# A decoder layer on one core: attention maxima by blocks of 64 queries for two heads at once, and two small stages taken through memory

## The chip, the cores and the metric

The kernel runs on one core of one Trainium2 chip. The metric is the device time of one execution in microseconds, from three executions without a profiler; a separate execution was taken with the hardware profiler, and every duration below that is not one of those three times comes from it. Engines are named as the profile names them: PE is the matmul engine, DVE the vector engine, ACT the scalar engine, POOL the general engine, and SP the queue that issues most of the transfers.

## The reference

One decoder layer works on x of 16 batches, 128 rows and 512 columns, in three sub-layers, each with a residual and a LayerNorm behind it. The retention part takes the 128 rows of a batch as the sequence. In the cross part a batch is read as 512 positions with 128 features. The last part picks 16 of the 128 rows of each batch.

```python
# 1. retention, 16 heads of 32, by batch
Q, K, V = (einsum('bsh,nhd->bnsd', X, W) for W in (W_Q, W_K, W_V))
ret = einsum('bnsd,bntd->bnst', xpos(Q), xpos(K, inverse)) * D      # D: gamma^(n-m), causal
Y = einsum('bnst,bntv->bnsv', ret, V)
Yn = (Y - mean) / sqrt(var + 1e-5) * gn_weight + gn_bias            # mean, var by head and row
x = layernorm(x + (silu(X @ W_G) * Yn) @ W_O)
# 2. banded attention over 512 positions, 8 heads of 16, |i - j| <= 64
scores = where(band, einsum('bqhd,bkhd->bhqk', q, k) / 4, lowest)
o = einsum('bhqk,bkhd->bqhd', softmax(scores), v) @ w_out.T + b_out
x = layernorm(x + relu(o).T * ctx @ w_ct + b_ct)
# 3. mixture of depths: 16 rows of each batch by score, then attention and MLP on those 256 rows
_, idx = top_k(einsum('btd,d->bt', x, w_router), 16); idx = sort(idx)
sel = x[b, idx]                                     # 256 rows
x1 = sel + causal_attention(rms_norm(sel))          # 16 heads, 8 key heads, rotary by idx
processed = x1 + (silu(h2 @ w_gate) * (h2 @ w_up)) @ w_down
x = layernorm(x.at[b, idx].set(gate * processed + (1 - gate) * sel))
```

## The kernel before, in words

All matmuls are fp32. Each shows as two records in the trace, so a count of records is twice the count of matmuls in the code.

**Three stages.** Retention goes by group, two batches at a time (8 groups). The cross part goes by batch, and inside a batch by unit: a unit is one batch with four of its eight heads (32 units; `m` is `2 * n + hg`). When retention has ended, the weights of the last part are loaded into a ring of six tiles, and that part runs on the 256 chosen rows.

**The order.** Each step is a generator with stages between its `yield`s. The tables `PLACES`, `ENDS`, `FIRST` and `ONCE` give a time to every stage of every step, and `in_order` sorts them into one order of the program. `FF_PLACES` does this for the last part. Each engine and each queue runs its own instructions strictly in that order, so the tables only decide what stands ahead of what.

**PSUM.** There are eight banks, handed out by `bank()` in rotation. The call that comes eighth after another gets its bank again, and waits until it has been read.

**The steps that matter here.** `scores` (steps `s0`, `s1`) computes, for a unit, the scores of two of the four chunks of 128 queries against the 192 or 256 keys in their band, for four heads in the four strips of 32 rows of PE. DVE adds the band and keeps the maximum of each query (L788): one instruction for one chunk and one head, so 8 behind each step and 16 for a unit. `lower` (step `low`) turns the maxima round and puts them, as one more feature, into the free rows of the queries `x_qT`: for batches 2 to 12 (`IN_MEMORY`) through two transfers, for batches 0, 1, 13, 14 and 15 by four transposes on PE (`xmx_ps`) from `wide_mxs`, which DVE has written directly. `weights` (steps `w0`, `w1`) then computes the transposed scores less their maxima, ACT takes the exponential (L829), and POOL cuts the band out (L835). `attend` (step `av`) multiplies with the values, `divide` and `turn` divide by the sums, `project_out` and `settle` finish the batch and write the score of each row.

In retention `variance` (step `var`) makes one divisor for each row and head. `normalise` (step `norm`) spreads it over the 32 features of a head by eight small matmuls into four banks (`spread_ps`, L708) and applies weight, bias and gate in eight DVE instructions (L712, L714). `finish` (steps `O0`, `O1`) multiplies by W_O.

`rank` counts, for each row of a batch, how many scores are above it: PE spreads the scores over the partitions by a transpose (`rank_ps`, L949), DVE compares and counts, a matmul with `after` numbers the chosen rows (`slot_ps`, L960), and DVE writes a 0/1 matrix into `wide` (L964), with which `gather` picks rows on PE.

At the start, SP issues the weights and, among the loads that follow, 25 small ones of the cross part; POOL issues only the four transfers of the decay table; the table `xpos` comes on ACT's queue.

Of the kernel before, what the change touches and what calls it, by code (L numbers as in the profile page):

```python
# [14 lines left out]
P = 128  # L15
# [6 lines left out]
GB = 2  # L22
# [12 lines left out]


IN_MEMORY = range(2, 13)
FREE = (XD, 0)
# [16 lines left out]
for _k, _w in _W.items():  # L55
# [7 lines left out]
    "q": [(-1.5107, 0.5513), (-1.4314, 0.6844)],  # L63
    "k": [(-1.51, 0.6571), (-1.4782, 0.7507)],
    "s0": [(-1.2644, -0.8382, 1.0251, 1.8751)],
    "s1": [(-0.6502, -0.1387, 1.1361, 2.4268)],
    "low": [(-0.452, 0.2528, 1.4558, 2.6592), (-0.3388, 0.255, 1.477, 2.6843)],
    "w0": [(0.351, 0.9575, 1.9746, 3.1188), (0.6532, 1.3693, 2.8463, 3.2972)],
    "w1": [(0.1628, 1.8596, 2.3575, 3.7432), (0.8299, 2.0241, 2.8359, 3.8093)],
    "av": [(1.0536, 2.2471, 3.077, 4.2619)],  # L70
    "div": [
        (1.549, 2.3132, 3.3032, 4.5514),
        (2.1607, 2.8293, 3.6961, 4.7908),
        (2.2814, 2.9057, 4.2425, 4.8691),
        (2.7316, 3.2963, 4.2834, 5.4207),],
    "v": [(-0.7717, 1.6867)],
    "enc": [(4.2298, 5.8947)],
    "turn": [(3.7073, 5.9438)],
    "out": [(5.5379, 6.1922), (5.6383, 6.7827)],
    "settle": [(5.7824, 7.2066), (6.1581, 7.7192), (6.2045, 8.378), (6.8636, 9.2875)],  # L80
    "rank": [(8.8254, 11.7601), (10.5726, 15.5543), (14.3738, 16.7912)],
    "load": [(-10.091,)],
    "Q0": [(-8.0888,), (-7.0032,)],
    "K0": [(-9.2641,), (-7.4284,)],
    "V0": [(-7.4999,)],
    "Q1": [(-6.8478,), (-6.0577,)],
    "R0": [(-6.7213,), (-6.147,)],
    "K1": [(-6.3248,), (-4.7817,)],
    "V1": [(-5.4583,)],
    "Y0": [(-5.0578,)],  # L90
    "G0": [(-4.829,), (-4.8109,)],
    "R1": [(-4.766,), (-4.6504,)],
    "G1": [(-4.5788,), (-4.5641,)],
    "Y1": [(-4.274,)],
    "var": [(-4.1573,), (-3.7966,)],
    "norm": [(-3.5102,)],
    "O0": [(-3.0724,), (-2.8181,), (-2.079,)],
    "O1": [(-2.0994,), (-0.2461,), (-0.0548,)],
# [4 lines left out]
        "q": [(-14.5047, -14.0322), (-9.6551, -10.8844)],  # L103
        "k": [(-14.6216, -0.0686), (-11.7977, 0.2659)],
        "s0": [(-10.3426, -9.3436, 0.6635, 1.6471)],
        "s1": [(-1.4102, -0.8775, 1.1056, 2.0571)],
        "low": [(-0.9192, 0.4442, 1.3301, 2.655), (25.4644, 25.2394, 26.846, 30.099)],
        "w0": [(-0.0687, 0.9881, 1.867, 3.6646), (0.6483, 1.0316, 2.1657, 3.801)],
        "w1": [(-0.716, 0.5784, 1.6289, 3.7788), (-0.1082, 0.8202, 2.3021, 4.2159)],
        "av": [(0.8022, 1.6738, 3.6998, 4.4162)],  # L110
        "div": [
            (1.3197, 2.3014, 3.8551, 4.5595),
            (9.3024, 12.4358, 15.7006, 13.259),
            (11.4285, 19.3987, 23.3186, 13.7145),
            (24.0753, 30.3386, 24.8529, 51.4762),],
        "v": [(-2.6646, -1.1793)],
        "enc": [(-25.1063, 5.5925)],
        "turn": [(3.2132, 5.214)],
        "out": [(3.4449, 5.6355), (4.2463, 5.7715)],
        "settle": [(4.6796, 7.6854), (5.8827, 7.8003), (6.6518, 8.4034), (6.7825, 8.7614)],  # L120
        "rank": [(8.7442, 12.5945), (11.2119, 15.6141), (14.4792, 18.3604)],
# [13 lines left out]
        "var": [(-3.6239,), (-3.5616,)],  # L135
        "norm": [(-3.4454,)],
        "O0": [(-3.0951,), (-2.9746,), (-2.0282,)],
        "O1": [(-2.7016,), (-2.0346,), (-1.7197,)],
    },
    1: {  # L140
        "q": [(-1.8166, -0.2185), (-1.7211, 0.2268)],
        "k": [(-1.4245, 0.5821), (-1.1045, 0.6675)],
        "s0": [(-1.1449, -0.3061, 1.1186, 0.88)],
        "s1": [(-0.7336, -0.1968, 1.3979, 1.5727)],
        "low": [(-0.299, 0.2134, 1.5144, 2.0884), (0.0557, 0.6188, 1.7807, 2.2233)],
        "w0": [(0.2707, 1.1081, 2.008, 3.7721), (0.3399, 1.2959, 2.8815, 3.7842)],
        "w1": [(0.4634, 0.7763, 2.1476, 3.124), (0.6199, 0.7887, 2.7228, 3.773)],
        "av": [(0.9363, 1.4927, 2.9839, 4.1957)],
        "div": [
            (0.9666, 1.6683, 3.2221, 4.4914),  # L150
            (1.3326, 2.19, 3.2714, 4.7046),
            (1.848, 2.4848, 3.3512, 5.1111),
            (2.0714, 3.0715, 4.4949, 5.7185),],
        "v": [(-2.1434, 1.2462)],
        "enc": [(2.2681, 6.6251)],
        "turn": [(3.7868, 6.1403)],
        "out": [(4.4181, 6.4823), (5.3138, 7.1825)],
        "settle": [(5.9958, 7.5759), (6.474, 7.966), (6.642, 8.7653), (7.2408, 8.9043)],
        "rank": [(10.0834, 11.6296), (12.019, 14.0816), (14.7883, 15.0275)],
        "load": [(-45.4451,)],  # L160
        "Q0": [(-40.5376,), (-31.555,)],
        "K0": [(-44.4545,), (-33.577,)],
        "V0": [(-28.6881,)],
        "Q1": [(-29.5172,), (-17.2537,)],
        "R0": [(-24.1539,), (-17.035,)],
        "K1": [(-32.7547,), (-24.7952,)],
        "V1": [(-13.608,)],
        "Y0": [(-9.3686,)],
        "G0": [(-20.8822,), (-15.6663,)],
        "R1": [(-7.9384,), (-5.8625,)],  # L170
        "G1": [(-8.5881,), (-7.538,)],
        "Y1": [(-5.1994,)],
        "var": [(-4.9466,), (-4.3898,)],
        "norm": [(-3.5502,)],
        "O0": [(-3.2591,), (-2.5035,), (-2.4622,)],
        "O1": [(-2.4561,), (-1.8438,), (-0.69,)],
    },
    6: {
        "q": [(-2.0548, 0.7039), (-2.0286, 0.9716)],
        "k": [(-1.5582, 0.6681), (-1.2975, 0.7797)],  # L180
        "s0": [(-1.1563, -0.4807, 0.9293, 1.876)],
        "s1": [(-0.9454, 0.0322, 1.3978, 2.4624)],
        "low": [(-0.5199, 0.3687, 1.8114, 2.9216), (0.1135, 0.7655, 6.6942, 8.7044)],
        "w0": [(0.619, 1.6449, 2.4026, 3.8245), (1.4903, 1.8685, 3.442, 3.9205)],
        "w1": [(0.4016, 1.312, 1.9452, 3.2547), (0.8685, 1.8118, 2.9524, 3.6025)],
        "av": [(1.5506, 2.0007, 3.7283, 4.366)],
        "div": [
            (1.7326, 2.5114, 4.5357, 5.4752),
            (2.3608, 3.0019, 14.1691, 12.0944),
            (2.6919, 3.5211, 32.2671, 26.848),  # L190
            (3.3016, 3.6721, 45.677, 30.3915),],
        "v": [(0.897, 3.5685)],
        "enc": [(3.2024, 5.2296)],
        "turn": [(3.8903, 5.8957)],
        "out": [(4.2266, 6.4601), (5.1506, 6.8067)],
# [14 lines left out]
        "Y1": [(-4.6408,)],  # L210
        "var": [(-4.088,), (-3.7221,)],
        "norm": [(-3.551,)],
        "O0": [(-3.1254,), (-3.0228,), (-2.9897,)],
        "O1": [(-2.7332,), (-2.301,), (-1.3014,)],
    },
    7: {
# [1187 lines left out]
```

## Time and profile before

| | |
|---|---|
| three executions without a profiler | 855.94, 855.16, 853.21 us; median 855.16 |
| the profiled execution | 857.26 us, of which the span from first to last instruction is 855.56 us |
| busy: PE, DVE, ACT, POOL | 825.2, 529.4, 384.8, 367.2 us |
| mean granted clock of PE | 0.987 |
| 50 to 548 us: PE busy | 497.6 of 498.0 us |
| 548 to 657.5 us: PE busy | 95.5 of 109.5 us |
| maxima on DVE (L788) | 512 of them, 424 ns for 256 columns and 357 ns for 192, each with a readout of 83 ns |

How to read it: a line of a group names the source line, the engine, the operation, what it writes and reads, the shape, how many records there are, how long they were busy together, the mean of one in ns, and the idle time of the engine just before them with what ended it. PE's records overlap, since matmuls are pipelined, so the cost of a step on PE is read from one start to the next. The span's parts are these: start to about 50 us, then retention and cross part interleaved until the last W_O matmul ends at 562.3 us, then the cross part alone until the second gather ends at 657.5 us, and then the last part.

### The profile page before, as it was taken

The page shows a single profiled execution, that of the slowest core. Times are in us where ns is not written, and L with a number is a line of the kernel's source. Part 1 is how long each engine was busy: PE and PEld are TensorE (multiplying, and loading weights), DVE is VectorE, ACT ScalarE, POOL GpSimd, SP SyncE. Part 2 cuts the span into 40 slices and gives each one's busy share as a digit, 9 for nine tenths or more (in the row PEclk, how much of TensorE's full clock was granted, in tenths as well). Part 3 has the DMA queues.
Part 4 walks back from the last instruction along what each step waited for, and adds up shares of the span by engine and source line. Part 5 has one row for each costly group of instructions (what it writes and reads, how often), then busy time and mean ns, then how long its engine had stood idle before and what let it go on. Part 6 is the DMA issues. An engine that isn't in the chain of part 4 may idle for free.

```text
span 855.6 us, 17846 instructions
## 1 busy us (share of the span) xinstructions
PE 825.2 (96%) x6762; PEld 571.1 (67%) x6762; DVE 529.4 (62%) x1793; ACT 384.8 (45%) x773; POOL 367.2 (43%) x527
## 2 busy tenths in 40 slices
PE   8999999999999999999999999988988999999996
PEld 6676767766766676587567657554554777658865
DVE  4644665677687678777787788877775276311112
ACT  0315634654473564546465456655443367421100
POOL 4634353364486554755654584644452121000001
PEclk9999999999999999999999999998899999999998
DMA  9500100003102110201211011138010633142500
GB/s 291 178 28 1 51 1 2 3 3 80 51 6 77 37 46 28 78 28 34 85 42 30 27 47 38 41 91 306 27 38 13 197 98 100 52 146 99 186 11 25
DMA packets 38373, 58.16 MB, mean 68 GB/s; under 512 B 10016, under 2 KB 13856, under 8 KB 38288
## 3 DMA queue, kind: packets, MB, share of 16 engines
q1 hardware_dynamic: 35552, 54.67, 19.9%
q10 hardware_dynamic: 2448, 1.58, 0.7%
q8 instruction: 53, 0.87, 0.4%
q0 software_dynamic: 288, 0.79, 0.3%
q14 instruction: 32, 0.26, 0.1%
HBM read 51.58 MB, written 5.44 MB: 67 GB/s over the span
## 4 chain that ended last, share of the span: by engine, by line
PE 81%; DVE 6%; issue 5%; DMA 3%; ACT 2%; POOL 1%; SPq 1%; POOLq 0%; DVEq 0%; ACTq 0%
PE xt_ps L824 7%; PE o_ps L722 7%; PE gu_ps L1248 7%; PE xs_ps L776 6%; PE xav_ps L846 6%; PE q_ps L604 6%; PE k_ps L604 6%; PE v_ps L623 6%; PE g_ps L632 6%; PE down_ps L1263 3%; PE wo_ps L1223 3%; PE xqk_ps L744 3%; PE xout_ps L904 2%; PE ret_ps L653 2%; PE xct_ps L914 2%
## 5 line engine op out<-in xcount | busy, mean ns | idle before, releaser
L788 DVE CUSTOM_DVE_ANT_0 x_masked<-xs_ps,x_band 128x192 f32<-128x192 f32 (+1 forms) x512 | 199.8, 390 | 73.0 <-PE xs_ps L776 34.0
L835 POOL TENSOR_SCALAR_AFFINE_SELECT xp_t<-xp_t 128x512 f32<-128x512 f32 (+1 forms) x256 | 146.2, 609 | 110.7 <-ACT xp_t L829 99.2
L829 ACT ACTIVATE xp_t<-xt_ps 128x448 f32<-128x448 f32 x256 | 118.6, 554 | 56.4 <-PE xt_ps L824 55.2
L776 PE MATMUL xs_ps<-x_kT,x_qT 32*128 32x192 f32 (+1 forms) x1024 | 71.9, 369 | 5.0 <-DVE x_masked L953 2.8
L824 PE MATMUL xt_ps<-x_qT,x_kT 32*128 32x192 f32 (+1 forms) x1024 | 71.5, 380 | 1.4 <-DVE x_qT L802 1.4
L824 PEld LDWEIGHTS xt_ps<-x_qT,x_kT 32*128 32x128 f32 x1024 | 48.0, 188 | 30.6 <-issue 14.8
L776 PEld LDWEIGHTS xs_ps<-x_kT,x_qT 32*128 32x128 f32 x1024 | 51.5, 186 | 20.4 <-issue 7.7
L663 POOL TENSOR_SCALAR_AFFINE_SELECT rt<-rt 128x2048 f32<-128x2048 f32 x16 | 32.5, 2029 | 66.5 <-ACT rt L658 66.5
L604 PE MATMUL q_ps<-xT,w_W_Q 128*128 128x256 f32 x256 | 59.4, 384 | 0.7 <-DMA xT<-in_xT 0.7
L604 PE MATMUL k_ps<-xT,w_W_K 128*128 128x256 f32 x256 | 58.8, 383 | 0.6 <-DMA w_W_K<-in_W_K 0.4
L632 PE MATMUL g_ps<-xT,w_W_G 128*128 128x256 f32 x256 | 59.1, 385 | 0.0
L722 PE MATMUL o_ps<-w_W_O,y 128*128 128x512 f32 x128 | 58.3, 599 | 0.0
L623 PE MATMUL v_ps<-w_W_V,xT 128*128 128x512 f32 x128 | 58.3, 599 | 0.0
L846 PE MATMUL xav_ps<-xp_t,x_va 128*32 128x192 f32 (+1 forms) x1024 | 57.1, 365 | 0.0
L604 PEld LDWEIGHTS q_ps<-xT,w_W_Q 128*128 128x128 f32 x256 | 47.6, 190 | 11.1 <-DMA xT<-in_xT 1.5
L604 PEld LDWEIGHTS k_ps<-xT,w_W_K 128*128 128x128 f32 x256 | 47.8, 190 | 10.7 <-issue 3.2
L632 PEld LDWEIGHTS g_ps<-xT,w_W_G 128*128 128x128 f32 x256 | 47.5, 190 | 9.3 <-issue 1.1
L658 ACT COPY rt<-ret_ps 128x512 f32<-128x512 f32 x64 | 32.9, 599 | 38.6 <-PE ret_ps L653 38.5
L846 PEld LDWEIGHTS xav_ps<-xp_t,x_va 128*32 128x32 f32 x1024 | 31.6, 112 | 25.0 <-issue 6.1
L1075 POOL TENSOR_TENSOR other<-other,ff_sin 128x512 f32<-128x512 f32 x12 | 15.6, 1306 | 64.7 <-ACT other L1072 53.4
L722 PEld LDWEIGHTS o_ps<-w_W_O,y 128*128 128x128 f32 x128 | 23.3, 190 | 27.4 <-issue 22.8
L623 PEld LDWEIGHTS v_ps<-w_W_V,xT 128*128 128x128 f32 x128 | 23.5, 190 | 26.3 <-issue 24.7
(214 smaller groups left out, 1473.3 us busy)
## 6 DMA issues: line engine op xcount, KB each, us to landing
x_rb<-inv_d SPq DMA_DIRECT2D x22, 256.0 KB
xp<-in_x SPq DMA_DIRECT2D x16, 256.0 KB
enc<-in_ctx SPq DMA_DIRECT2D x16, 256.0 KB
out<-z_plain SPq DMA_DIRECT2D x16, 256.0 KB
wq<-in_wq SPq DMA_DIRECT2D x4, 1024.0 KB
wo<-in_wo SPq DMA_DIRECT2D x4, 1024.0 KB
w_gate<-in_w_gate SPq DMA_DIRECT2D x4, 1024.0 KB
w_up<-in_w_up SPq DMA_DIRECT2D x4, 1024.0 KB
```

What stands on the lines that cost most here:

```text
L604: nc.tensor.matmul(ps[:, i * GT:(i + 1) * GT], w[wname][:, kc, hg * P:(hg + 1) * P], st["xT"][:, kc, :], start=(kc == 0), stop=(kc == KC - 1))
L623: nc.tensor.matmul(ps, state[g]["xT"][:, kc, b * S:(b + 1) * S], w["W_V"][:, kc, :], start=(kc == 0), stop=(kc == KC - 1))
L632: nc.tensor.matmul(ps[:, i * GT:(i + 1) * GT], w["W_G"][:, kc, hg * P:(hg + 1) * P], state[g]["xT"][:, kc, :], start=(kc == 0), stop=(kc = ...
L658: nc.scalar.copy(rt[:, j].rearrange("p g b s -> p (g b s)"), sc[j])
L722: nc.tensor.matmul(ps, st["y"][:, kc, b * S:(b + 1) * S], w["W_O"][:, kc, :], start=(kc == 0), stop=(kc == KC - 1))
L776: nc.tensor.matmul(ps[j][:, OFF[c]:OFF[c] + LEN[c]], qT[hs, c * P:(c + 1) * P], kT[hs, LO[c]:LO[c] + LEN[c]], start=True, stop=True)
L788: nc.vector.tensor_tensor_reduce(out=junk[:, 0:LEN[c]], in0=ps[j][:, OFF[c]:OFF[c] + LEN[c]], in1=band[:, SEEN[c]:SEEN[c] + LEN[c]], scale ...
L824: nc.tensor.matmul(ps[j][:, OFF[c]:OFF[c] + LEN[c]], kT[hs, c * P:(c + 1) * P], qa[hs, LO[c]:LO[c] + LEN[c]], start=True, stop=True)
L829: nc.scalar.activation(p[:, j, :], ps[j][:, 0:448], AF.Exp, scale=XD ** -0.5)
L835: nc.gpsimd.affine_select(out=v, in_=v, pattern=[[0, 4], [sign, b - a]], base=a if sign == 1 else P - a, channel_multiplier=-sign, compare ...
L846: nc.tensor.matmul(ps[32 * j:32 * (j + 1), LO[c]:LO[c] + LEN[c]], va[:, c, hg * 4 + j, :], p[c // 2][:, j, OFF[c]:OFF[c] + LEN[c]], start= ...
L1248: nc.tensor.matmul(ps[:, j * n:(j + 1) * n], loaded[f"{w}{q}"][:, kc, at:at + P], ff["x1", "T"][:, kc, lo:hi], start=(kc == 0), stop=(kc = ...
```

## The change

The names in brackets are those of the steps in the order.

- **Scores by 64 queries of two heads.** The queries of both head groups lie side by side, 64 and 64, in one tile `x_qT` of 8 blocks. One matmul takes 128 stationary columns that are 64 queries of one head and the same 64 queries of a second, against the 128 (first and last block) or 192 keys of their band. A batch has 8 blocks by 4 strips, so 32 matmuls as before, in three parts of 3, 2 and 3 blocks (`s0`, `s1`, `s2`) and with 12 bank calls for 16. The keys are needed once with all rows (`x_kA`) and, for `weights`, once for each head group (`x_kT`), made by ACT from `x_kA`: three ACT instructions for two.
- **`low` by batch.** Batches 2 to 12 write the maxima once and read them twice, 33 transfers for 44. The other five batches copy the maxima into `x_wide_mx` in two halves one after the other, POOL for the lower 64 partitions and DVE for the upper, each with four transposes and a DVE addition.
- **Retention's divisors through memory** for groups 1 to 6: written by SP, read back spread over 128 partitions (512 KB) into the tile `sq`; then one DVE multiplication over 1024 columns, four ACT instructions for weight and bias, and a second DVE multiplication for the gate, in place of eight matmuls and eight DVE instructions.
- **Ranks of batches 2 to 12 through memory:** the score is written and read back to all partitions, 22 transfers for 11 transposes. **Slots for two batches** at once: 8 matmuls for 16.
- **Small loads** of the cross part by POOL: 18 transfers, some of them joined, in place of 25 on SP; `xpos` moves from ACT's queue to SP's, behind the first quarter of the weights.
- **Buffers:** the score's product in `settle` is written to `z_plain` (one buffer, also that of the output), not to `x_masked`; `turn` uses the `xu` tiles.
- **All times in the tables are new**, so the order of nearly all steps shifts.

```diff
-    "s0": [(-1.2644, -0.8382, 1.0251, 1.8751)],
-    "s1": [(-0.6502, -0.1387, 1.1361, 2.4268)],
+    "s0": [(-1.5639, 0.8804)],
+    "s1": [(-0.9647, 1.0899)],
+    "s2": [(-0.8135, 1.4413)],
-    "var": [(-4.1573,), (-3.7966,)],
-    "norm": [(-3.5102,)],
+    "var": [(-4.6497,), (-4.6403,), (-4.5439,)],
+    "norm": [(-3.8842,), (-3.5722,)],
...
+NB, HB = D // BAND, BAND
+B_LO = [max(b * HB - BAND, 0) for b in range(NB)]
+B_LEN = [min(b * HB + HB + BAND, D) - B_LO[b] for b in range(NB)]
+PARTS = (0, 3, 5, NB)
+SPREAD_IN_MEMORY = range(1, 7)
...
         def xload(name, shape):
-            nc.sync.dma_start(out=v, in_=t[name])
+            nc.gpsimd.dma_start(out=v, in_=t[name])
...
-        nc.scalar.dma_start(out=xpos, in_=t["consts"][:, XPOS[0]:XPOS[1]].rearrange(
+        nc.sync.dma_start(out=xpos, in_=t["consts"][:, XPOS[0]:XPOS[1]].rearrange(
...
         def variance(g):
             nc.vector.reciprocal(rs, rs)
+            if g in SPREAD_IN_MEMORY:
+                rs_d = dram.tile([16, 4 * GB, S], F32, name="rs_d")
+                nc.sync.dma_start(out=rs_d.rearrange("k n s -> n k s"), in_=rs)
+                yield
+                nc.sync.dma_start(
+                    out=st["sq"].rearrange("p g n -> p (g n)"),
+                    in_=bc(rs_d.rearrange("k n s -> k (n s)")[0:4], 1, HD))
...
         def normalise(g):
+            if g in SPREAD_IN_MEMORY:
+                y = st["y"]
+                nc.vector.tensor_tensor(y, y, st["sq"], ALU.mult)
+                for hg in range(4):
+                    nc.scalar.activation(y[:, hg, :], y[:, hg, :], AF.Identity,
+                                         bias=gnb[:, hg:hg + 1], scale=gnw[:, hg:hg + 1])
+                yield
+                nc.vector.tensor_tensor(y, y, st["gate"], ALU.mult)
+                return
...
-        def scores(m, half):
+        def scores(n, part):
+            q, k = cross[n]["q"], cross[n]["k"]
+            blocks = [(b, sum(B_LEN[PARTS[part]:b])) for b in range(*PARTS[part:part + 2])]
+            for b, off in blocks:
                 for j in range(4):
                     hs = slice(32 * j, 32 * (j + 1))
-                    nc.tensor.matmul(ps[j][:, OFF[c]:OFF[c] + LEN[c]],
-                                     qT[hs, c * P:(c + 1) * P],
-                                     kT[hs, LO[c]:LO[c] + LEN[c]],
+                    nc.tensor.matmul(ps[j][:, off:off + B_LEN[b]],
+                                     q[hs, b].rearrange("p e r -> p (e r)"),
+                                     k[hs, B_LO[b]:B_LO[b] + B_LEN[b]],
                                      start=True, stop=True)
...
         def lower(n):
             if n not in IN_MEMORY:
+                for half in range(2):
+                    for e, engine in enumerate((nc.gpsimd, nc.vector)):
+                        rows = slice(e * HB, (e + 1) * HB)
+                        engine.tensor_copy(
+                            wide[rows, :, :, FREE[e]],
+                            mx[rows].rearrange("p (j h b) -> p h j b", j=4, h=2)[:, half])
+                    ps = bank("xmx_ps")
+                    for i in range(4):
+                        nc.tensor.transpose(ps[:, i * P:(i + 1) * P],
+                                            wide_mx[:, i].rearrange("p j w -> p (j w)"), ident)
+                    at = q[:, 4 * half:4 * half + 4].rearrange("p b e r -> p (b e r)")
+                    nc.vector.tensor_tensor(at, at, ps, ALU.add)
                 return
...
         def rank(n):
+            if n in IN_MEMORY:
+                every = xk.tile([P, P], F32, name="x_every", bufs=2)
+                nc.sync.dma_start(out=every, in_=cross.pop(("score", n)).rearrange(
+                    "p one -> one p").partition_broadcast(P))
+                yield
...
+        def slot(g):
+            both = slice(GB * g, GB * g + GB)
+            ps = bank("slot_ps")
+            nc.tensor.matmul(ps[:, 0:GB], cc["after"], chosen[:, both], start=True, stop=True)
```

## The prediction

> **What bounds the kernel now.** I read the busy shares first, then stretches of the span, then groups and single starts.
>
> ```profile
> PE 825.2 (96%) x6762; PEld 571.1 (67%) x6762; DVE 529.4 (62%) x1793; ACT 384.8 (45%) x773; POOL 367.2 (43%) x527
> ```
>
> The stretches (length, then busy time of PE, weight loads, DVE, ACT, POOL, clock, DMA share, GB/s) say where that 96% lies:
>
> ```profile
> 50.00:548.00 498.00, 497.60 (x4763) 337.49 (x4765) 360.49 (x1252) 263.37 (x484) 264.79 (x372) 1.00 0.12 35
> 548.00:562.30 14.30, 13.26 (x132) 7.58 (x127) 12.15 (x47) 9.35 (x18) 11.02 (x19) 1.00 0.15 45
> 562.30:617.50 55.20, 47.90 (x462) 29.00 (x461) 40.99 (x166) 26.84 (x53) 25.15 (x46) 0.88 0.45 153
> 617.50:657.50 40.00, 34.30 (x269) 21.58 (x267) 26.52 (x80) 18.22 (x42) 18.04 (x32) 0.96 0.11 34
> ```
>
> From 50 to 548 us PE never stops, so matmul time taken out there is time gained, as long as nobody makes PE wait. From 562.3 us (last W_O matmul) the cross part is alone; PE waits, mostly for DVE, and its clock drops:
>
> ```profile
> 575.83 0.59 PE L776 MATMUL xs_ps<-x_kT,x_qT 32*128 32x192 f32 x4
> 579.21 1.86 PE L776 MATMUL xs_ps<-x_kT,x_qT 32*128 32x192 f32 x12 [2.79 <-DVE x_masked L953]
> 581.00 2.08 PE L904 MATMUL xout_ps<-xo,x_w_outT 128*128 128x512 f32 x2
> 583.00 1.88 PE L824 MATMUL xt_ps<-x_qT,x_kT 32*128 32x192 f32 x16
> ```
>
> Here xout takes 2.0 us from start to start, elsewhere 0.96: a wait is paid again in clock. The groups that the change touches:
>
> ```profile
> L776 PE MATMUL xs_ps<-x_kT,x_qT 32*128 32x192 f32 (+1 forms) x1024 | 71.9, 369 | 5.0 <-DVE x_masked L953 2.8 <-DVE x_wide_mx L788 1.6 <-ACT x_kT L747 0.4
> L708 PE MATMUL spread_ps<-gn_rs,spread 32*128 32x128 f32 x128 | 10.5, 292 | 0.2 <-DVE gate L641 0.2
> L949 PE MATMUL rank_ps<-consts,score 128*128 128x128 f32 x16 | 4.7, 291 | 0.9 <-DVE score L932 0.7 <-DVE x_wide_mx L788 0.2
> ```
>
> **The change part by part.** Busy times of PE overlap, so I price steps from start to start in the timeline:
>
> ```profile
> 301.69 1.17 PE L653 MATMUL ret_ps<-ret_qT,ret_kT 32*128 32x128 f32 x32
> 302.69 0.94 PE L776 MATMUL xs_ps<-x_kT,x_qT 32*128 32x256 f32 x16
> 303.55 3.72 PE L632 MATMUL g_ps<-xT,w_W_G 128*128 128x256 f32 x16
> 307.11 1.02 PE L914 MATMUL xct_ps<-xy,x_w_ct 128*128 128x512 f32 x2
> ```
>
> *Scores.* g_ps: 3.56 us for 8 matmuls of 256 columns, 1.74 ns a column. A call of scores has 448 columns in each strip, 0.78 us; its median from start to start over the 63 calls that stand alone is 0.97 us, so 0.19 us are overhead. A batch has four calls: 3.88 us. After: parts of 512, 384 and 512 columns, 0.89, 0.67 and 0.89 us and three overheads: 3.04 us. Saved 0.84 x 16 = **13.4 us**. The Trainium skill speaks against this (TensorE: Matmul & The Clock Gate, LDWEIGHTS): a load of 32 rows costs as much as one of 128, the columns of the stationary side count. The change has as many loads as before; if they set the pace, the saving is 0. But retain's row is the test: 16 matmuls of 128 columns in 1.00 us (median 1.10), 0.069 us each, against 0.121 for 224 columns on average. That is 0.54 ns a column in both: time goes with moving columns. I take the row.
>
> *Divisors.* Eight matmuls of spread_ps take 0.8 us by starts; six groups: **4.8 us**. *Ranks and slots.* 0.21 us each; 11 + 8 fewer: **4.0 us**. PE loses 22.2 us.
>
> *Start, +1.2.* R0 waits for POOL:
>
> ```profile
> 1.43 2.45 POOL L465 DMA_DIRECT2D y<-in_decay  x4 [0.53 <-issue]
> 11.51 1.77 POOL L486 TENSOR_TENSOR table_q<-gate,y 128x512 f32<-128x512 f32 x1 [7.49 <-DMA gate<-in_consts]
> 22.50 0.98 PEld L653 LDWEIGHTS ret_ps<-ret_qT,ret_kT 32*128 32x128 f32 x32 [0.36 <-POOL ret_kT L616]
> ```
>
> Four issues took 2.45 us on POOL, 0.61 each; 18 more now stand ahead of table_q: 3.9 + 11.0 = 15 us, not 11.5. Then two tables and four rotary steps, 8.6 us: 23.7 for 22.5. Bounds: 0 (issues shorter) to 3 (0.3 MB more among the weights). SP loses 25 loads, but xT of group 1, issued at 36.08 before, held PE only 0.2 us: 0.
>
> *`low` in halves, +2.4.* On DVE the second half's copy stands behind the first half's addition, which waits for the transposes; PE's next four transposes wait for that copy: 0.16 drain + 0.68 (addition) + 0.15 and handovers, 1.2 us in which PE stands. Twice (batches 0 and 1) in the full stretch; three times in the tail, below. No row shows it; 0.6 to 3 each, as POOL copies too.
>
> *Banks, +3.* A strip's bank is now read by three maxima, and four banks take 12 x 0.44 = 5.2 us to clear, not 3.8. I set the PE work between each call and the eighth bank call after it against that, batches 2 to 11: before, the spare time had a median of 2.2 us and was never below 0, and no wait shows; after, the median is 1.9 and four are -0.3 to -0.9. 2.6 us, a little more where DVE is late; 0 to 10.
>
> *Round trip of the divisors, 0.* Chain: root with its table 1.65, reciprocal 0.94, write to read 2.0 (L809 to L811), landing, multiply 1.74 (the rate of L524), ACT 4 x 0.45, multiply 1.74: 10.1 us plus landing. PE has 18.7, 21.3, 20.4, 20.4, 23.8 and 22.9 us of other work between var and O0 in groups 1 to 6. The nearest transfer is the spread reciprocal, 256 KB from four rows:
>
> ```profile
> 525.36 0.55 SPq L885 DMA_DIRECT2D x_rb<-inv_d  x1
> 530.57 0.75 DVE L888 SCALAR_TENSOR_TENSOR xu<-xu,x_ours,x_rb 128x512 f32<-128x512 f32 x1 [0.82 <-DMA x_rb<-inv_d]
> ```
>
> 5.2 us. For 512 KB that gives 5.2 to 10.4; I take 8. The Trainium skill (DMA: Bandwidth & Descriptors, Anatomy of one DMA - SWDGE (gpsimd) path, fitted for the general engine's transfers) has 2.0 us plus bytes at 436 GB/s: 3.2 us for 512 KB, and 2.6 where the trace has 5.2; the trace decides. By the rule the chain takes 13.3 us, by the trace 18.1: no wait on PE either way, but with 1 to 6 us spare, not 5 to 10. DVE reaches the multiply some 8 us after var and would stand 3 to 5 us. Behind it wait the next shuffle of q and its bank, wanted 8 us later. DVE can afford it: it is 72% busy in the full stretch and loses work: the maxima were 256 x 424 + 256 x 357 ns and become 384 x 357 + 128 x 290 (290 for 128 columns by the slope from 256 to 192), 199.9 to 174.2, **-25.7 us**; normalise 4.74 to 3.5 in six groups, -7.5.
>
> *At nothing:* ACT gets 16 more key copies (0.78) and 24 more of normalise (0.45), +23 us to 408, still under half; but `attend` follows its last `weights` by 5.6 us of PE work in some batches where it was 6.1, and exponentials and cuts take 4 x 0.554 + 4 x 0.609 = 4.7. Cover 0.9 us. SP: +12 +22 -11 -25 = -2 transfers. Ranks have over 10 us to come back; if late, DVE stands. The score's product waits for the last output's landing (`z_plain`), 15 us of PE work away, some 5 in the last three batches; 0 to +1 each. The moving queries of `weights` now lie in runs of 64: rope_ps (L996) reads runs of 16 and takes 0.22 us for 128 columns, as fav_ps (L1212) does for contiguous ones. Order in the last part: same 110 us of steps priced alike, +-0.5.
>
> *Tail, -1.* Before, 36.8 us of PE work lie between the last W_O and the last xmx, in 55.2 us. After, retention ends earlier and 41.2 us lie there. DVE sets the pace: 76 maxima of 0.423 (32), 2.5 settles (9), additions and copies (4.5), ranks, rows and divisions (9): 54.5, and three stands for xmx of 1.5: 59. That is 18 us of waiting, as before. To the second gather: 31.0 in 40.0 before; 31.8 and about 10 after, since the last rank follows xct with only 1 us of cover for 4.6 (frot stood there), while gather0 now covers xout to xct: +1. The 2 us of waiting at 548 to 562 fall to the tail's sum: -2.
>
> **Sum:** -22.2 + 1.2 + 2.4 + 3 + 0 - 1 = -16.6. The profiled execution took 857.26 us (span 855.56 and 1.7 around it): 840.7. The median of the runs is 2.1 lower: **838.6 us**.
>
> **The rivals.** *More of it* (830): DVE's relief shortens the tail by 5 and banks cost nothing. For: PE waits there for L788. Against: more maxima are left after the last W_O. *Less of it* (849): 19 of 30 parts have under 2 us of spare bank time; if DVE is late by a microsecond at half of them, and attend's cover fails, +10. *Loads set the pace after all* (852): 838.6 + 13.4; the change then does not do what it says. Against: retain. *Slower*: the landing of the 512 KB. At 13.9 us the six groups are late by 5.3, 2.7, 3.6, 3.6, 0.2 and 1.1, 16.5 in sum, and the gain is gone; at 16 us they are late by 29: 868. Against: 5.2 us for half the bytes, and longer rows. For: SP issues in order, so the read also waits behind whatever SP waits for (its waits for DVE ran to 77 us in the trace).
>
> **How the numbers follow.** Likeliest 0.42, more 0.22, less 0.22, loads 0.06, slower 0.08. About 0.3%, 2.6 us, is what can be told from no change here: under 852.6 is faster. Faster: 0.42 + 0.22 + 0.22 + 0.02 of the loads' case = 0.88; same 0.04; slower 0.08. The range runs from the larger gain with a cheap start (825) into the smaller gain with dear bounds (851).
>
> **What would show it.** Right: xs_ps at about 58 us for 71.9, spread_ps with a quarter of its records, PE still without gaps from 50 us to the last W_O, which ends near 537. Wrong: gaps before xmx in batches 0 and 1 absent, gaps at O0 of groups 1 to 6 (slower), waits for x_masked between 100 and 500 us (less), part calls of 1.3 us and more (loads).

## The result, and the profile after

The changed kernel takes 919.72 us (median of four executions, 918.79 to 922.95) where the kernel before takes 855.43 beside it: 1.0764 of before, 95% interval 1.0730 to 1.0797. The forecast was 838.6 us, range 825 to 851. PE's busy time has not fallen, and its idle time has trebled: 30.4 us of the span before, 92.9 after (first the busy shares of the page, then stretches: length, busy time of PE, weight loads, DVE, ACT and POOL, granted clock, DMA share, GB/s):

```profile
PE 824.4 (90%) x6639; PEld 568.1 (62%) x6639; DVE 496.4 (54%) x1749; ACT 405.5 (44%) x813; POOL 381.2 (42%) x552
```

```profile
50.00:583.00 533.00, 497.23 (x4672) 335.40 (x4670) 327.00 (x1208) 281.55 (x519) 264.46 (x367) 0.97 0.17 39
583.00:666.40 83.40, 55.34 (x574) 34.81 (x574) 47.30 (x201) 36.24 (x70) 38.55 (x73) 0.82 0.35 114
666.40:716.20 49.80, 38.24 (x248) 18.46 (x247) 28.94 (x81) 16.19 (x31) 20.58 (x39) 0.83 0.10 34
```

Up to the last W_O matmul (583 us) PE stands for 36 us, where before it stood 0.4 between 50 and 548. From there to the second gather (716 us) it took 133 us for 95. The granted clock is lower where the gaps are: 0.97, 0.82, 0.83. The parts that were to shrink did (groups after, one line for each of the three):

```profile
L831 PE MATMUL xs_ps<-x_kA,x_qT 32*128 32x192 f32 (+1 forms) x1024 | 61.2, 336 | 11.3 <-DVE x_mx L839 7.2 <-issue 1.8 <-ACT xp_t L891 1.1
...
L745 PE MATMUL spread_ps<-gn_rs,spread 32*128 32x128 f32 x32 | 1.5, 296 | 0.0
...
L839 DVE CUSTOM_DVE_ANT_0 x_masked<-xs_ps,x_band 128x192 f32<-128x192 f32 (+1 forms) x512 | 174.3, 341 | 72.7 <-PE xs_ps L831 40.2 <-DVE x_mx L839 0.5
```

What has grown stands in the waits (engine and line, what it waited for: us in total, times, longest). After:

```profile
ACT y L736 <- DVE y L734: 45.4, 6, 9.5
...
DVE xu L950 <- DMA x_rb<-inv_d: 35.8, 8, 9.5
POOL xy L971 <- DMA enc<-in_ctx: 34.8, 5, 14.7
...
DVE y L734 <- DMA sq<-rs_d: 32.0, 5, 8.8
...
PE xt_ps L886 <- DMA x_qT<-x_mT_d: 20.3, 5, 7.9
```

and before, where the other three kinds do not occur:

```profile
POOL xy L908 <- DMA enc<-in_ctx: 12.1, 2, 11.0
...
DVE xu L888 <- DMA x_rb<-inv_d: 6.6, 6, 2.8
```

Four of the five are waits for transfers; ACT's is for DVE, which stands for one. Only two of them (`sq` and ACT's wait behind it) go back directly to a transfer that the change added. PE's 20.3 us are for the maxima's read-back, which is in both kernels. One stretch of the timeline after shows how:

```profile
477.65 0.33 SPq L1000 DMA_DIRECT2D own_d<-score  x1
478.10 0.35 SPq L944 DMA_DIRECT2D inv_d<-x_r  x1
...
479.65 0.61 SPq L723 DMA_DIRECT2D rs_d<-gn_rs  x1
...
488.05 0.57 SPq L725 DMA_DIRECT2D sq<-rs_d  x1
...
488.71 0.51 SPq L917 DMA_DIRECT2D sum_d<-xu  x1
...
489.32 0.55 SPq L947 DMA_DIRECT2D x_rb<-inv_d  x1
489.92 0.67 SPq L869 DMA_DIRECT2D x_mT_d<-x_mT  x1
495.86 0.31 SPq L940 DMA_DIRECT2D x_r<-sum_d  x1
498.35 0.75 DVE L950 SCALAR_TENSOR_TENSOR xu<-xu,x_ours,x_rb 128x512 f32<-128x512 f32 x1 [9.46 <-DMA x_rb<-inv_d]
498.70 1.13 SPq L873 DMA_DIRECT2D x_qT<-x_mT_d  x2
...
500.66 1.58 ACT L736 ACTIVATE y<-y,col_gn_bias,col_gn_weight 128x256 f32<-128x256 f32 x3 [9.50 <-DVE y L734]
...
501.48 1.01 PE L886 MATMUL xt_ps<-x_qT,x_kT 32*128 32x192 f32 x7 [7.91 <-DMA x_qT<-x_mT_d]
```

The reader is to follow SP downwards. A write of 128 scores (`own_d`) is issued at 477.65. The divisors' write, two microseconds behind it, is read back only at 488.05, since it had not landed sooner. The 512 KB of `sq` then stand ahead of `sum_d`, `x_rb` and the write of the maxima (`x_mT_d`), which lands 8.7 us after its issue, so that SP can issue their reads only at 498.70. DVE, ACT and PE stand 9.5, 9.5 and 7.9 us.

Below, a landing is the time from a transfer's issue to the last update of its semaphore in the trace. In the changed kernel the eleven writes `own_d` land after 8.4 us (median; 7.8 to 11.6), and `inv_d` close behind one of them after 7.7 to 9.5, else after 1.4 (median). The six reads `sq` land after 9.5 (median; 7.6 to 12.4), and `x_qT` issued while one of them is under way after 5.7 to 12.0, else after 2.0 (median). The waits of SP itself say the same (after; then before):

```profile
SPq L947 <- DMA inv_d<-x_r: 19.0, 11, 5.9
...
SPq L725 <- DMA rs_d<-gn_rs: 15.5, 6, 7.7
...
SPq L940 <- DMA inv_d<-x_r: 9.4, 3, 7.4
```

```profile
SPq L885 <- DMA inv_d<-x_r: 11.6, 15, 1.6
```

### The profile page after: what moved, and what is told of

Read it like the earlier page. It is cut to its first block, busy times and chain, and to the rows that moved or that the text cites. A ratio compares the mean times of both kernels' runs of the same rounds, so it can differ in the third digit from the quotient of the medians.

```text
span 917.3 us, 17612 instructions
## 1 busy us (share of the span) xinstructions
PE 824.4 (90%) x6639; PEld 568.1 (62%) x6639; DVE 496.4 (54%) x1749; ACT 405.5 (44%) x813; POOL 381.2 (42%) x552
## 5 line engine op out<-in xcount | busy, mean ns | idle before, releaser
L839 DVE CUSTOM_DVE_ANT_0 x_masked<-xs_ps,x_band 128x192 f32<-128x192 f32 (+1 forms) x512 | 174.3, 341 | 72.7 <-PE xs_ps L831 40.2
L897 POOL TENSOR_SCALAR_AFFINE_SELECT xp_t<-xp_t 128x512 f32<-128x512 f32 (+1 forms) x256 | 143.2, 598 | 113.3 <-ACT xp_t L891 109.5
L886 PE MATMUL xt_ps<-x_qT,x_kT 32*128 32x256 f32 (+1 forms) x1024 | 74.2, 387 | 21.6 <-DMA x_qT<-x_mT_d 20.3
L886 PEld LDWEIGHTS xt_ps<-x_qT,x_kT 32*128 32x128 f32 x1024 | 50.6, 192 | 45.7 <-issue 34.2
L908 PE MATMUL xav_ps<-xp_t,x_va 128*32 128x192 f32 (+1 forms) x1024 | 63.8, 390 | 13.4 <-POOL xp_t L897 13.2
L831 PE MATMUL xs_ps<-x_kA,x_qT 32*128 32x192 f32 (+1 forms) x1024 | 61.2, 336 | 11.3 <-DVE x_mx L839 7.2
L831 PEld LDWEIGHTS xs_ps<-x_kA,x_qT 32*128 32x128 f32 x1024 | 50.8, 197 | 20.6 <-DVE x_mx L839 8.5
L839 DVE DVE_READ_ACCUMULATOR2_ANT x_mx<- 128x1 f32 x512 | 42.5, 83 | 0.2
```

The lines of the kernel that those rows point to most:

```text
L831: nc.tensor.matmul(ps[j][:, off:off + B_LEN[b]], q[hs, b].rearrange("p e r -> p (e r)"), k[hs, B_LO[b]:B_LO[b] + B_LEN[b]], start=True, st ...
L839: nc.vector.tensor_tensor_reduce(out=junk[:, 0:B_LEN[b]], in0=ps[j][:, off:off + B_LEN[b]], in1=band[:, B_SEEN[b]:B_SEEN[b] + B_LEN[b]], s ...
L886: nc.tensor.matmul(ps[j][:, OFF[c]:OFF[c] + LEN[c]], kT[hs, c * P:(c + 1) * P], qa[hs, LO[c] // HB:(LO[c] + LEN[c]) // HB], start=True, st ...
L897: nc.gpsimd.affine_select(out=v, in_=v, pattern=[[0, 4], [sign, b - a]], base=a if sign == 1 else P - a, channel_multiplier=-sign, compare ...
L908: nc.tensor.matmul(ps[32 * j:32 * (j + 1), LO[c]:LO[c] + LEN[c]], va[:, c, hg * 4 + j, :], p[c // 2][:, j, OFF[c]:OFF[c] + LEN[c]], start= ...
```

## The experiments

All are variants of the changed kernel. Each ratio is to the kernel before on the same chip, with its 95% interval; the changed kernel stands at 1.0764.

| variant | ratio to before | interval |
|---|---|---|
| divisors on PE | 1.0443 | 1.0410 to 1.0476 |
| ranks on PE | 1.0241 | 1.0192 to 1.0289 |
| both on PE | 1.0051 | 1.0034 to 1.0067 |
| divisors by ACT's queue | 1.0719 | 1.0679 to 1.0760 |
| ranks on PE, divisors by ACT's queue | 1.0261 | 1.0218 to 1.0305 |
| divisors on PE, ranks by ACT's queue | 1.0408 | 1.0361 to 1.0455 |
| both on PE, the ranks' writes kept | 1.0315 | 1.0268 to 1.0361 |
| divisors on PE, ranks' writes of 128 bytes | 1.0082 | 1.0055 to 1.0109 |
| ... and small loads by SP | 1.0129 | 1.0106 to 1.0152 |
| ... and `low`'s second copies by POOL | 1.0111 | 1.0088 to 1.0135 |
| ... small loads by SP, divisors read later | 1.0550 | 1.0521 to 1.0578 |
| ... small loads by ACT, `low` by POOL | 1.0075 | 1.0050 to 1.0099 |
| ranks' writes of 128 bytes, divisors read from 16 rows | 1.0057 | 1.0035 to 1.0079 |
| divisors on PE, reciprocals from 16 rows, `low` by POOL | 1.0077 | 1.0055 to 1.0100 |
| both reads from 16 rows, `low` by POOL | 1.0017 | 1.0000 to 1.0034 |
| ... and small loads by SP behind group 1 | 0.9934 | 0.9914 to 0.9953 |

**Which part.** The first theory was that the divisors' read stands ahead of the maxima in SP's queue.

```diff
-SPREAD_IN_MEMORY = range(1, 7)
+SPREAD_IN_MEMORY = ()
```

> The kernel after with retention's divisors spread by PE again in all groups, as before; all times in the tables unchanged. Theory A (the 512 KB read-back of the divisors stands in SP's queue ahead of the maxima's read-back, and PE waits for the maxima): the five waits of PE for x_qT at 193, 270, 349, 427 and 501 us (3.6, 2.3, 3.2, 3.3, 7.9; 20.3 in sum) go, and DVE's 32 us of standing at the multiplication; 48 matmuls come back, +4.8. 919.7 - 20.3 - some 5 of lowered clock behind each wait + 4.8: 895 to 903. Theory B (the wider maxima and the new order make PE wait by themselves; the divisors only show where it waits): PE then waits elsewhere, 912 to 925.

```diff
             if n in IN_MEMORY:
-                every = xk.tile([P, P], F32, name="x_every", bufs=2)
-                nc.sync.dma_start(out=every, in_=...)
                 yield
-            else:
-                every = bank("rank_ps")[:, 0:P]
-                nc.tensor.transpose(every, own.to_broadcast([P, P]), ident)
+            every = bank("rank_ps")[:, 0:P]
+            nc.tensor.transpose(every, own.to_broadcast([P, P]), ident)
```

> The kernel after with the ranks of batches 2 to 12 by a transpose on PE again (at the place of the second stage), 22 transfers fewer. Theory A: the full stretch keeps its waits; the ranks' transfers (128 pieces of 4 bytes) hold up what is issued behind them in the last 100 us only a little: 914 to 921. Theory C (the ranks' transfers delay inv_d, rs_d and enc behind them, 5 to 8 us at a time, and this is most of the loss between the last W_O and the second gather): the stretch 583 to 716 us shortens by 10 to 20, total 900 to 910.

Both edits together:

> The kernel after with both the divisors and the ranks back on PE; scores by 64 queries, slots for two batches and small loads by POOL stay. Theory A: near the kernel with the divisors alone put back, 892 to 903; if the two losses add up with theory C, 878 to 890. Theory B: above 905. In every theory the scores keep their 61 us of PE time against 72 before.

Measured: 891.7, 872.8 and 859.5 us. All three lie below every range that was given for them. The divisors are worth 28 us with the ranks in memory and 13 without; the ranks 47 with the divisors in memory and 32 without. Theory A, which gave the ranks next to nothing, had the smaller half. Theory C saw the ranks' loss only behind the last W_O matmul. There lies half of it: from that matmul to the second gather 133 us become 109. The other half lies ahead, where the last W_O ends at 559.9 us for 583.0. The divisors' 28 us lie all ahead of it (555.2 us; behind it 133 us as before). With the ranks on PE the writes of the divisors land in 2.1 us each time, and SP's waits shrink:

```profile
SPq L947 <- DMA inv_d<-x_r: 12.9, 10, 2.6
...
SPq L725 <- DMA rs_d<-gn_rs: 6.1, 6, 1.5
```

**Is it SP's queue?** Three runs moved transfers to ACT's queue.

```diff
-                nc.sync.dma_start(out=rs_d.rearrange("k n s -> n k s"), in_=rs)
+                nc.scalar.dma_start(out=rs_d.rearrange("k n s -> n k s"), in_=rs)
                 yield
-                nc.sync.dma_start(
+                nc.scalar.dma_start(
                     out=st["sq"].rearrange("p g n -> p (g n)"),
```

> The kernel after with the divisors still through memory, but both of their transfers issued by ACT, so on ACT's queue and not ahead of the maxima's read-back in SP's. Theory A in its queue form (transfers of one queue land in the order of their issue): the waits of PE for x_qT fall to 1 us or less each, DVE still stands at the multiplication, 897 to 907. If what counts is the bytes that share the 16 DMA engines whatever the queue: x_qT is still late by 2 us or more in each group, 912 to 921.

The same edit with the ranks on PE:

> Ranks on PE, divisors through memory with both transfers on ACT's queue; to be read against the run with ranks on PE and the divisors on SP's queue (872.8) and the one with both on PE (859.5). If the divisors cost their 13 us by standing ahead of other transfers in SP's queue: the waits of PE for x_qT go and the time is 860 to 866 (DVE still stands at the multiplication). If it is the bytes in the shared DMA engines, or DVE's standing: 869 to 875.

With the divisors on PE, `own_d` and `x_every` on ACT's queue (the same kind of edit):

> Divisors on PE, ranks through memory with both transfers on ACT's queue; to be read against 891.7 (same, on SP's queue) and 859.5 (both on PE). Theory D (a write of 128 pieces of 4 bytes lands only after about 8 us, and every transfer that SP issues behind it lands after it): off SP's queue it holds up nothing that PE needs, 857 to 866. Theory E (the write slows all DMA work, or the ranks themselves come too late): 878 to 893.

Measured: 917.0, 875.8 and 888.5: no gain, or next to none (919.7, 872.8 and 891.7 on SP's queue). The queue form of the theory falls. In the last of the three, three writes `inv_d` on SP, issued 0.5 us behind an `own_d` on ACT's queue, still land after 7.6 to 8.0 us; in the second, `x_qT` at 257 us on SP lands after 8.3 and 9.9 us behind an `sq` on ACT's. What is held up is what the transfers share, not the order of one queue. The Trainium skill (DMA: Bandwidth & Descriptors, Queues, rings and completion order) says why that can be: both queues put their work on the same 16 DMA engines, and an engine's semaphore write lands only after every earlier write of that engine, across its queues. The landings agree with it.

**Is it the write?** Both on PE; the scores are still written and never read.

```diff
+            if n in IN_MEMORY:
+                own_d = dram.tile([P, 1], F32, name="own_d")
+                nc.sync.dma_start(out=own_d, in_=score[:, n:n + 1])
```

> Divisors and ranks on PE; the 11 writes of 128 scores stay on SP's queue, and nobody reads them (an addition that the result does not need). Theory D: the writes alone make the loss, 882 to 893, inv_d behind them lands after 8 us for 1.4. If the loss comes from the read-back or from DVE waiting for the ranks: 859 to 864.

Then the ranks through memory, but with pieces of 128 bytes: DVE turns the scores by 32 x 32 first.

```diff
-                nc.sync.dma_start(out=own_d, in_=score[:, n:n + 1])
+                turned = small.tile([P, 32], F32, name="score_T", bufs=1)
+                nc.vector.transpose(turned, score)
+                nc.sync.dma_start(out=own_d.rearrange("(a r) one -> a (r one)", r=32),
+                                  in_=turned[n::32, :])
```

> Divisors on PE; the ranks go through memory on SP's queue, but DVE first turns the scores by 32 x 32, so that a write is 4 pieces of 128 bytes, not 128 of 4 bytes. Theory D with the size of a piece as the cause: the write lands in about 1.5 to 2 us, time 855 to 862. If any further write and read in SP's order costs that much: 880 to 893.

Measured: 879.2 and 858.9. Against both on PE (1.0051), the dead writes alone cost 2.6 of the 3.9 points (per cent of the time before) that the ranks through memory cost, somewhat less than theory D gave them. They land after 7.7 us, DVE waits for `x_rb` in the same way as in the changed kernel (20.7 us here, 2.4 with both on PE and no writes), and SP for `inv_d`:

```profile
DVE xu L950 <- DMA x_rb<-inv_d: 20.7, 7, 6.9
...
SPq L947 <- DMA inv_d<-x_r: 24.7, 12, 4.8
```

With 4 pieces of 128 bytes in place of 128 of 4 bytes the write lands after 1.6 us, and the loss is gone as far as can be told, read-back included (1.0082 against 1.0051, whose intervals overlap). The write also occupies fewer DMA engines then: its semaphore gets 5 updates, not 16. No run changed one without the other, but other writes in the trace after narrow it: `inv_d`, 32 pieces of 256 bytes, also gets 16 updates and lands after 1.4 us, and `x_mT_d`, 128 pieces of 128 bytes, lands after 2.0. So neither 16 updates nor 128 pieces make 8 us by themselves. What is left is the piece of 4 bytes, or that pieces of many engines lie within the same 512 bytes; these two stay unseparated.

**The divisors: place or engines?** First the place, with the small loads of the start moved too (below): the divisors of groups 2 to 5 are read behind the maxima and multiplied later.

```diff
-SPREAD_IN_MEMORY = ()
+SPREAD_IN_MEMORY = range(2, 6)
...
-    "var": [(-4.6497,), (-4.6403,), (-4.5439,)],
-    "norm": [(-3.8842,), (-3.5722,)],
+    "var": [(-4.6497,), (-4.6403,), (-4.02,)],
+    "norm": [(-3.45,), (-3.3,)],
```

> As the first run of this call, but with the divisors of groups 2 to 5 through memory again, read back behind the maxima's read-back (var's third stage at -4.02 for -4.5439) and multiplied later (norm at -3.45 and -3.30 for -3.88 and -3.57). If only the meeting of the two reads cost time: PE waits for no x_qT, and 32 matmuls fewer give -2 to -4 us against the first run. If 512 KB hurts wherever it lies (DVE stands at the multiplication, other transfers of SP land late): 0 to +8.

898.4 us, 35 above its base (863.7), a miss for both theories. The maxima now land in 1.9 us in three of the four groups, but the 512 KB still take 7.5 to 11.3, and the later place has waits of its own. The timeline of this variant:

```profile
203.50 1.22 DVE L735 TENSOR_TENSOR y<-y,sq 128x1024 f32<-128x1024 f32 x1
204.76 2.07 ACT L737 ACTIVATE y<-y,col_gn_bias,col_gn_weight 128x256 f32<-128x256 f32 x4 [5.03 <-DVE y L735]
206.74 0.56 ACT L914 COPY xu<-xav_ps 128x512 f32<-128x512 f32 x1
...
207.36 0.90 PE L928 MATMUL xut_ps<-consts,xu 128*128 128x128 f32 x3 [5.86 <-ACT xu L914]
```

ACT has its four instructions of `norm` in order too: they stand behind DVE's multiplication, and the copy that PE's transposes need stands behind them (5.86 us of PE). What part of the 35 us this makes was not measured.

The update counts then pointed to the cause. `sq` gets 5 updates of its semaphore, one about 1.0 us after its issue and four together at the end; `enc`, a load to 128 rows, gets 16. The Trainium skill (DMA: Bandwidth & Descriptors, Rules for kernel authors) says that a transfer whose outermost dimension has fewer than 16 rows runs on at most that many DMA engines; a broadcast from 4 rows then runs on 4, which fits the four late updates. So the divisors are written four times and read from 16 rows, at the same bytes (together with the 128-byte pieces):

```diff
-                rs_d = dram.tile([16, 4 * GB, S], F32, name="rs_d")
-                nc.sync.dma_start(out=rs_d.rearrange("k n s -> n k s"), in_=rs)
+                rs_d = dram.tile([16, 4, 4 * GB, S], F32, name="rs_d")
+                for c in range(4):
+                    nc.sync.dma_start(out=rs_d[:, c].rearrange("k n s -> n k s"), in_=rs)
...
-                    in_=bc(rs_d.rearrange("k n s -> k (n s)")[0:4], 1, HD))
+                    in_=bc(rs_d[0:4].rearrange("k c n s -> (k c) (n s)"), 1, HD // 4))
```

> Divisors through memory as in the kernel after, but written four times, so that the 512 KB are read from 16 rows and not from 4; ranks' writes in 128-byte pieces. To be read against divisors on PE (1.0082 of before) and against ranks on PE with the divisors read from 4 rows (1.0241). The semaphore of the read from 4 rows gets 5 updates where that of a load to 128 rows gets 16. Theory F (4 rows run on 4 DMA engines only, and these then hold up what others write): the read lands in 3 to 6 us for 9.8, PE's waits for x_qT and ACT's 30 us of standing go, ratio 1.000 to 1.010. Theory G (512 KB take that long however they are cut): 1.020 to 1.028.

The cross part's reciprocals in the same way, with the divisors on PE:

> Divisors on PE, ranks' writes in 128-byte pieces, low's second copies by POOL (about 1.006 of before by the sum of two runs), and the cross part's reciprocals written four times and read from 16 rows (256 KB, 5.0 us from 4 rows). Theory F: x_rb lands in 2.5 to 3.5 us; DVE stood only 2 us for it in this base, so the time changes by 0 to -2: 1.003 to 1.007. The 66 further issues on SP could cost as much: up to 1.012.

Both:

> Both reads from 16 rows, with low's second copies by POOL: the kernel after with every transfer mended and nothing put back on PE but nothing else changed. Theory F: the first run of this call less 2 us, 0.997 to 1.008. Theory G: 1.018 to 1.026.

Measured: 858.3, 860.0 and 854.5. In the first of the three `sq` gets 16 updates and lands after 4.9 us (median; 4.5 to 6.3) for 9.5, in the second `x_rb` after 3.2 for 5.0. `x_qT` lands within 4.1 us in the first, PE does not wait for it, and the waits of `norm` there are these:

```profile
ACT y L738 <- DVE y L736: 18.4, 6, 4.9
...
DVE y L736 <- DMA sq<-rs_d: 12.1, 4, 5.5
```

With the ranks on PE and the read from 4 rows they were 30.0 and 30.1 us. Theory F had ACT's wait go altogether; it only shrank. The rule and the runs agree: the same 512 KB from 16 rows take half the time. That leaves the divisors through memory no dearer than on PE (1.0057 against 1.0082). The reciprocals alone gain nothing that can be told, since DVE waits little for them there. With the divisors in memory too, they and `low`'s copies together gain 3.8 us, where 2 were expected (1.0057 to 1.0017).

**The start and `low`.** On the variant with the divisors on PE and 128-byte writes, the 18 small loads went back to SP, behind the weights, and `xpos` to ACT's queue:

```diff
-            nc.gpsimd.dma_start(out=v, in_=t[name])
+            nc.sync.dma_start(out=v, in_=t[name])
...
-        nc.sync.dma_start(out=xpos, in_=...)
+        nc.scalar.dma_start(out=xpos, in_=...)
```

> The kernel with the divisors on PE and the ranks' writes of 128-byte pieces (1.0082 of before), with the 18 small loads back on SP and xpos back on ACT's queue. If the issues by POOL and the loads ahead of the weights make the start late (PE stood 2.3 to 3.4 us at R0 at 25.5 us where before it stood 0.4 at 22.5): R0 at 22.5 to 23.5, ratio 1.002 to 1.005. If the start is late for another reason (order of K, Q, R0): ratio 1.007 to 1.009.

Then `low`'s second copies by POOL on top:

```diff
-                    for e, engine in enumerate((nc.gpsimd, nc.vector)):
+                    for e, engine in enumerate((nc.gpsimd, nc.gpsimd if half else nc.vector)):
```

> As the run above it, and the second half's copies of the maxima in low both by POOL, so that none stands behind DVE's addition. If DVE's order is what keeps PE at xmx (1.7 and 2.5 us in batches 0 and 1, three times 1.1 in the tail): each wait falls to 0.5 to 1.0, in all 2 to 4 us, ratio 0.998 to 1.002. If the wait is for PE's own transposes and the handovers: within 1 us of the run above.

and the loads by ACT's queue instead, with the same `low`:

> Divisors on PE, ranks' writes in 128-byte pieces (1.0082 of before), the 18 small loads and xpos on ACT's queue, whose engine has little to do before 20 us, and the second half's copies in low by POOL. In the run with the loads back on SP, R0 started at 21.3 us, 4.5 earlier than with POOL's issues, but xT of group 1 stood behind the loads and PE waited 9.3 us for it. If both can be had on ACT's queue: R0 at 21 to 23 and no wait for xT, -3 to -4.5, and -1.8 from low: 851 to 857 against a before of 853, ratio 0.999 to 1.005. If ACT's own first work becomes late: 1.006 to 1.010.

Measured: 863.7, 861.9 and 859.2 (1.0129, 1.0111, 1.0075); no ratio fell into the range given for a gain. In the first, R0, the first matmul of retention's scores, came at 21.3 us, earlier than the 22.5 to 23.5 expected, but the loads hold up xT of group 1 on SP:

```profile
21.29 1.17 PE L674 MATMUL ret_ps<-ret_qT,ret_kT 32*128 32x128 f32 x32
...
38.91 1.62 PE L625 MATMUL q_ps<-xT,w_W_Q 128*128 128x256 f32 x3 [9.34 <-DMA xT<-in_xT]
```

and on ACT's queue W_G lands late (PE waits 6.8 us for it at 29.1). PE's wait at `low` falls to 0.65 us in each of its five places with the new copies, from 1.7 and 2.5 us (batches 0 and 1) and some 1.1 (the last three) without them. The loads were last put on SP behind xT and x of group 1, where nothing that is needed soon stands behind them, on top of both reads from 16 rows:

```diff
+        def small_loads():
+            for out, in_ in later:
+                nc.sync.dma_start(out=out, in_=in_)
...
+    "small": [-800.0],
```

> As the run with both reads from 16 rows (1.0017 of before), with xpos on ACT's queue and the 18 small loads issued by SP behind xT and x of group 1. If the late start comes from POOL's issues ahead of its first table, and the 9.3 us wait of the earlier trial from xT standing behind the loads: R0 at 21 to 23 us for 25.8, no wait for xT over 1 us, -2.5 to -4.5 us, ratio 0.996 to 0.999. If weights or xT land too late for the earlier start anyway: 1.000 to 1.004.

848.1 us, 0.9934 of before, with the interval below 1: 0.7% less than the kernel before, and more than the 2.5 to 4.5 us that were expected (6.4 below 854.5). R0 starts at 20.7 for 26.1, the last W_O ends 5.9 us earlier, and there is no wait for xT:

```profile
20.67 1.17 PE L684 MATMUL ret_ps<-ret_qT,ret_kT 32*128 32x128 f32 x32
...
28.78 1.46 PE L635 MATMUL q_ps<-xT,w_W_Q 128*128 128x256 f32 x6
```

Its stretches, to be set against those of the changed kernel:

```profile
50.00:534.20 484.20, 477.21 (x4607) 323.92 (x4605) 326.85 (x1211) 277.60 (x514) 271.16 (x374) 1.00 0.16 47
534.20:600.80 66.60, 53.35 (x573) 33.25 (x574) 47.41 (x200) 36.19 (x70) 34.89 (x67) 0.85 0.41 144
600.80:647.50 46.70, 38.34 (x248) 18.78 (x247) 30.84 (x82) 16.24 (x31) 20.68 (x39) 0.85 0.11 36
```

## Why the prediction was wrong

The forecast was faster, the kernel is slower. Its terms for PE's own work held; two terms that it set at 0, the divisors' round trip and SP's transfers with the ranks, cost some 60 us, and the tail was mis-sized by some 12.

- **Scores, -13.4: right.** The parts of 512 and 384 columns take 1.07 and 0.87 us from start to start (medians), 3.0 a batch for 3.04 (the working's own parts add to 3.02). The loads of the stationary side did not set the pace. What the scores alone are worth to the whole kernel was not run. DVE's maxima went from 199.8 to 174.3 us, as worked out.
- **Divisors, ranks and slots on PE, -4.8 and -4.0: right.** The spread takes 0.68 us a group where it is on PE (4.1 for six), a rank 0.21, a slot 0.18.
- **Start, +1.2: too small.** The 18 issues by POOL kept its first table until 17.9 us, not 15: several waited for earlier ones to land, and R0 came at 25.8 for 22.5, +3.3, just beyond the bound of 3:

```profile
17.89 1.29 POOL L503 TENSOR_TENSOR table_q<-gate,y 128x512 f32<-128x512 f32 x1
...
25.84 1.45 PE L673 MATMUL ret_ps<-ret_qT,ret_kT 32*128 32x128 f32 x20 [3.15 <-POOL ret_kT L636]
```

- **`low` in halves, +2.4:** 1.73 and 2.46 us, 4.2 in all, by the mechanism named (DVE's copy behind its own addition): with that copy on POOL both are 0.65.

```profile
102.75 0.83 DVE L854 COPY x_wide_mx<-x_mx 64x16 f32<-64x16 f32 x1
...
103.72 0.63 PE L859 MATMUL xmx_ps<-consts,x_wide_mx 128*128 128x128 f32 x4 [1.73 <-DVE x_wide_mx L854]
```

- **Banks, +3:** PE's waits for maxima in the full stretch sum to 4.4 us after, and to 1.4 with the divisors on PE and 128-byte writes.
- **Round trip of the divisors, 0: the step that failed first.** Its landing of 8 us was near (9.5), its chain adds to 9.9 us and not 10.1, which changes nothing, and no O0 was late, as it said. But it asked only whether O0 and DVE could bear the landing. It did not ask what is issued behind 512 KB on four engines (the maxima's read-back: PE waited 20.3 us for it), and of the four ACT instructions a group it counted the work (24 of 0.45 us, 11 us) and not that they wait for DVE (45.4 us). Taking the divisors out of memory gave 28 us. DVE stood 6.4 us at each of five multiplications, not 3 to 5. The reason for the landing stood in the row it took the time from: 5.2 us for the 256 KB of `x_rb`, where `enc`, as large, lands in 2.9 us (median before). The prediction read that as the price of bytes; the run from 16 rows (3.2 us) shows that much of it is the price of four rows.
- **SP's transfers, "-2", and ranks "over 10 us to come back", 0: the step that cost most.** Transfers were counted by their issues. Eleven of them write 4 bytes 128 times, land after 8 us, and what is issued close behind lands late too. Taking the ranks out of memory gave 47 us. That the ranks themselves come back in time was nearly right (DVE waited for one, 5.1 us), and beside the point.
- **Tail, -1: mis-sized.** Mended in every transfer (1.0017), the kernel ends its last W_O at 540.1 us; 537 was forecast. From there to the second gather the prediction's own sums give 59 + 42 = 101 us; it takes 113.7 (95.2 before). In the fastest variant it is 66.6 + 46.7 = 113.3: PE is idle for 21.6 us (13.0 before) and busy for 9.5 us more than before, of which the larger work in the prediction's sums (73.0 for 67.8) accounts for 5.2. The clock is 0.85 there, for 0.88 and 0.96. PE's longest single wait is 5.0 us, of `attend` for POOL's cut; no other is above 2.5. With divisors and ranks back on PE the stretch still takes 107.7, so 12.5 of the 18 us above before are there without the transfers of either; no run took it further apart, and its cause stays open. A small slip lies there too: the waiting at 548 to 562 us, counted at 2 us, is 1.0 in the row shown.
- **The rivals.** "Slower" (chance 0.08) had the sign and one of the two right objects, the 512 KB, with the wrong path: it expected O0 to be late from a landing of 13.9 us. No read took that long. Its remark that SP issues in order pointed to the cause, but it was used for the divisors' own delay and not for what they delay.

## What to carry to other kernels

A small transfer is not priced by its own lateness: list what is issued behind it, on any queue, and who waits for that. Before a stage goes through memory, look at the pieces of its write and at the outermost rows of its read; here 128 pieces of 4 bytes and a broadcast from 4 rows took 61 us more (919.7 for 858.3) than 4 pieces of 128 bytes and 16 rows, at the same bytes read. When work is moved to another engine, count what its instructions wait for and what stands behind them: ACT's four instructions a group, 11 us of work in all, stood for 45 us.

## What the runs showed that was not expected

- The write of 128 scores, 512 bytes in all, lands after 8.4 us; the maxima's write of 16 KB in pieces of 128 bytes lands after 2.0. The sixteen semaphore updates come one after another over some 5 us (480.8 to 485.5 for the write of the scores at 477.65).
- A transfer on one queue delays the landing of another queue's: `inv_d` on SP lands after 7.6 to 8.0 us behind `own_d` on ACT's, else after 1.4.
- The number of a semaphore's updates in the trace (5 or 16) went with how wide a transfer runs: 256 KB to 128 partitions land after 5.0 us from 4 rows, 3.2 from 16.
